# Part of the early rows fetched by SP during the sums, fewer parked by POOL

## The chip, the cores and the metric

One core of one Trainium2 chip runs the whole program. The metric is the device time of one execution in microseconds, the median of the runs. The engines are TensorE (PE), VectorE (DVE), ScalarE (ACT), GpSimd (POOL) and SyncE (SP); each works through its own instructions in order and waits on semaphores for the others. Transfers are issued from SP, ACT and POOL.

## What is computed

A graph convolution with a residual, a mixture of 64 experts of which each node uses two, a norm over all nodes and a norm over each row. There are N = 12500 nodes with D = 256 features and M = 212500 edges, sorted by their target node.

```python
deg_out = clip(segment_sum(ones, src), 1); deg_in = clip(segment_sum(ones, dst), 1)
h = feats * rsqrt(deg_out)[:, None]
m = segment_sum(h[src], dst) * rsqrt(deg_in)[:, None]
x = m @ W_gc + b_gc + feats @ W_res + b_res
y = x + top2_experts(x)
z = (y - mean(y, 0)) * rsqrt(var(y, 0) + eps) * gamma + beta
out = layernorm(feats + z)          # over the features of a node
```

The change lies in the line that makes `m`: for every edge a row of `h`, at the number in `src`, is fetched and added to its target.

## The kernel before

**Stages.** First the degrees of all nodes are counted on PE from one-hot codes that DVE and ACT make. Then x is scaled row by row to `h` and stored in DRAM (`h_d`). Then come the sums over the edges, interleaved with the dense layer, the gating and 20 early tiles of experts. Then the experts, then the two norms.

**Groups of edges.** An edge's source row is fetched by an indirect DMA of POOL, 128 rows of 1 KB at a time; the code calls such a set of 128 edges a row (here: a *row*). There are 1416 rows (`MC`) that POOL gathers from `h_d` during the sums, into a ring of 20 places (L962, in the function `row`). PE multiplies each by a one-hot matrix that DVE made twelve rows ahead (L954, `one_hot`), and adds it into a window of 128 nodes (L976).

**Early rows.** Another 180 rows (`SC`), 90 pairs (`NC2`), are not gathered in the sums. POOL fetches their sources earlier, from x itself, because `h` is not known yet: 140 of them while the degrees are counted (`early_row`, L309), the other 40 right after (`parked`, L746), into 16 buffers of a pair each. SP stores each pair to DRAM (`early_d`, L320 and L773); the parked ones only after the 16 stores of h that stand ahead of them on SP's queue (L768, L770). With more than 16 pairs to park, POOL waits for buffers.

In the sums these pairs come back, one pair for every nine rows (`BATCH`). For a pair, `fetch_again` has SP send the numbers of its 256 sources to all partitions (L1713) and load the rows from `early_d` (L1717). As the rows were taken from x, each must still be multiplied with the scale of its source: DVE makes one-hot codes of the source's low digits (`digits`, L1722), PE looks the scales up (`look_up`, L1730), DVE picks the right one by the high digit (`factors`, L1738) and makes the one-hot codes of the targets (L1745), ACT scales the rows (`scaled`, L1755), and PE adds them up (`sum_again`, L1760). Two buffers alternate, so pair k + 2 is fetched when pair k has been summed.

**Accumulators.** `acc` holds the sums of all nodes, in 14 pieces (`NPW`). A piece is set to zero by SP, which copies zeros from DRAM (`cleared`, L1699; each clear first loads a register, L1692). Before the sums `acc` held x and h. The sums reach the pieces in the order of the nodes, so those of the last nodes are touched last.

**Order.** In the sums the order on PE, DVE, ACT, POOL and SP is written out by hand: `at_row(c, f)` puts a piece of work behind row c of all engines' lists, and each engine then takes its own instructions in that order. So a DMA of SP that is issued "at row 300" stands on SP's queue behind all that was put there before, and waits for nothing but its own semaphores and those ahead of it. Besides the early pairs, SP has there the rows of h that belong to a group's own nodes (`own`, L1002), the stores of finished nodes (L1148) and the weights of the early tiles (L1485). Between the stage of `h` and the sums there is a branch (L795) for inputs that do not fit the windows; it is not taken here. `take` and `hold` share PSUM buffers between the chains.

Of the kernel before, what the change touches and what calls it, by code (L numbers as in the profile page):

```python
# [11 lines left out]
I32 = mybir.dt.int32  # L12
U32 = mybir.dt.uint32
AF = mybir.ActivationFunctionType
ALU = mybir.AluOpType
# [4 lines left out]
P = 128  # L20
N = 12500
D = 256
# [24 lines left out]
HE = HC * P  # L47
BL = 26
# [3 lines left out]
MC = UG * GR  # L52
SR = 15
SB = 4
SG = SB * (NB - 1)
SC = SG * SR
# [3 lines left out]
L = -(-(M - HE - SC * P) // NL // 2) * 2  # L60
# [78 lines left out]
D2 = D + 2  # L139
# [5 lines left out]
def gnn_moe_kernel(  # L145
# [60 lines left out]
    lane = const.tile([P, P], F32)  # L206
# [60 lines left out]
    acc = accp.tile([P, 2 * NP], F32)  # L267
# [9 lines left out]
    src_col = edge.tile([P, NC], I32)  # L277
    rel = edge.tile([P, NC], F32)
# [20 lines left out]
    early = {"wait": []}  # L299
    STORE_LAG = 4  # L300

    def early_row(c):

        while early["wait"] and (early["wait"][0][0] <= c - STORE_LAG):
            stored()
        if c % 2 == 0:
            early["t"] = line.tile([P, 2, D], F32, name="early", bufs=6)
        t = early["t"]
        GP.indirect_dma_start(  # L309
            out=t[:, c % 2],  # L310
            out_offset=None,
            in_=x,
            in_offset=bass.IndirectOffsetOnAxis(ap=src_col[:, MC + c : MC + c + 1], axis=0),
        )
        if c % 2:
            early["wait"].append((c, t))

    def stored():
        c, t = early["wait"].pop(0)
        nc.sync.dma_start(early_d[c // 2], t)  # L320

    def early_rows(to):
        for c in range(early.get("n", 0), min(to, SC)):
            early_row(c)
        early["n"] = max(early.get("n", 0), min(to, SC))
        while early["n"] == SC and early["wait"]:
            stored()

    in_order = tc.manual_schedule(engines={mybir.EngineType.Pool, SP, DVE})
# [2 lines left out]
    with ExitStack() as stack:  # L332
# [226 lines left out]
        for c0 in range(0, C0 + 1, CH):  # L559
            n = min(CH, C0 + 1 - c0)  # L560
# [18 lines left out]
            for k in range(k0, k1):  # L579
                c = k * G  # L580
# [42 lines left out]
        c = C0 + 1 - rest  # L623
# [109 lines left out]
    with ExitStack() as stack:  # L733
# [110 lines left out]
    with ExitStack() as stack:  # L844
# [11 lines left out]
        for i in range(5):  # L856
            r = one.tile([P, RR, D2], F32, name=f"ring{i}")
# [3 lines left out]
        again_ = []  # L861
        for i in range(2):
            r = one.tile([P, 2, D2], F32, name=f"again{i}")
# [13 lines left out]
        p_again = banks[2][:, :D2]  # L877
# [789 lines left out]
        def at_row(c, f):  # L1667
            heapq.heappush(todo, (c, len(given_at), f))
            given_at.append(c)

        def compact_by(c):

            steps_of = squeeze_all()
            lays = [(j, which) for j in range(0, GR, 4) for which in range(2)]
            c -= 3 * len(lays) + 4 + 4 + NL * GR // P + 6
            for i, f in enumerate(steps_of):
                at_row(c * i / len(steps_of), lambda t, f=f: f())
            for i, (j, which) in enumerate(lays):
                at_row(c + 3 * i, lambda t, j=j, w=which: hold(t, lambda t: lay(j, w, t)))
            end = c + 3 * len(lays) + LAG  # L1680
            at_row(end, lambda t: cleared(range(NPW - 4, NPW)))
            for i in range(NB - 1):
                for j in range(NC2 // (NB - 1)):
                    k = i * (NC2 // (NB - 1)) + j
                    fetch_at.append(end + 4 + BATCH * k)
            for k in range(2):
                at_row(fetch_at[k], lambda t, k=k: fetch_again(k, t))

        def cleared(pieces):

            for i in pieces:
                _, u = nc.values_load_multi_w_load_instructions(  # L1692
                    unfit_i[0:1, 0:1],
                    engines=[SP],
                    min_val=0,
                    max_val=1,
                    skip_runtime_bounds_check_because="unfit_i is a comparison",
                )
                nc.sync.dma_start(  # L1699
                    acc[:, i * PW : (i + 1) * PW],  # L1700
                    acc_d[bass.ds(u[0] * (i + 1), 1)].rearrange("a p f -> p (a f)"),
                )
# [4 lines left out]
        def fetch_again(k, t):  # L1707

            i = k * 2
            b, j = divmod(i, SB * SR)  # L1710
            e = HE + b * BE + BL * L + j * P
            wide = spare[:, (3 + k % 2) * D : (4 + k % 2) * D]
            nc.sync.dma_start(  # L1713
                wide.bitcast(I32),
                src[e : e + 2 * P].rearrange("(a c) -> a c", a=1).to_broadcast([P, 2 * P]),
            )
            nc.sync.dma_start(again_[k % 2][:, :, :D], early_d[k])  # L1717
            at_row(t + 4, lambda t: digits(k, wide, t))

        def digits(k, wide, t):  # L1720
            w = wide.bitcast(I32)
            V.tensor_single_scalar(w, w, 127, op=ALU.bitwise_and)  # L1722
            V.tensor_scalar(wide, w, part, None, op0=ALU.is_equal)
            at_row(t + 2, lambda t: hold(t, lambda t: look_up(k, wide, t)))
# [26 lines left out]
        def scaled(k, wide, t):  # L1751
# [3 lines left out]
                S.activation(r[:, i, :D], r[:, i, :D], AF.Copy, scale=factor[:, c : c + 1])  # L1755
            at_row(t + 2, lambda t: sum_again(k, 0, wide, t))

        def sum_again(k, i, wide, t):
            g, j = divmod(2 * k + i, SR)
            T.matmul(  # L1760
                p_again, wide[:, i * P : (i + 1) * P], again_[k % 2][:, i],
                start=j == 0, stop=j == SR - 1,
            )
            if j == SR - 1:
                at_row(t + 2, lambda t: out_of(UG + g, t))
            if i == 1 and k + 2 < NC2:
                at_row(max(t + 1, fetch_at[k + 2]), lambda t: fetch_again(k + 2, t))
            if i == 0:
                if j == SR - 1:
                    at_row(t + 4, lambda t: sum_again(k, 1, wide, t))  # L1770
                else:
                    sum_again(k, 1, wide, t)

        with tc.manual_schedule(engines={
            mybir.EngineType.PE, DVE, mybir.EngineType.Activation, mybir.EngineType.Pool, SP,
        }):
# [15 lines left out]
            at_row(MC - 240, lambda t: x_part(0, t))  # L1792
            at_row(SORT_AT, sort_early)
            at_row(TAKE_AT - 16, lambda t: soon.update(close=True))
            for i in range(EARLY):
                at_row(TAKE_AT + STEP * i, lambda t, i=i: behind(
                    "gated", i - 2, t, lambda t, i=i: early_tile(i, t)
                ))
            compact_by(HC - AHEAD)
            for c in range(AHEAD):  # L1800
                one_hot(c)
            for c in range(MC):
                row(c)
                if c + AHEAD < MC:
                    one_hot(c + AHEAD)
                while todo and todo[0][0] <= c:
                    heapq.heappop(todo)[2](c)
            for i in range(AT_ONCE):
                tc.declare_no_dep(
                    add_early(i, at_e[:, 1]).ins,  # L1810
                    group="late stores",
                    reason="nodes of early tiles were ranked before",
                )
            while todo:
                t, _, f = heapq.heappop(todo)
                f(t)
# [16 lines left out]
    with ExitStack() as stack:  # L1833
# [14 lines left out]
            junk, left, cnt, None, op0=ALU.is_gt, op1=ALU.add, accum_out=pos[:, 0:1]  # L1848
# [23 lines left out]
    with ExitStack() as stack:  # L1872
# [204 lines left out]
        n = EARLY - AT_ONCE  # L2077
# [320 lines left out]
```

## Time and profile before

| | us |
|---|---|
| median of 3 runs | 3549.48 |
| the three runs | 3547.8, 3549.48, 3579.87 |
| the profiled execution | 3578.71 |
| its span, first to last instruction | 3576.9 |
| parking, first to last gather of POOL | 359.03 to 418.93 |
| first product of the sums on PE | 440.51 |
| last gather of the sums starts | 2583.7 |
| busy: PE / PE loads / DVE / ACT / POOL | 2494.7 / 1898.2 / 1797.0 / 826.2 / 2186.7 |

Times in the profile are microseconds from the first instruction, unless marked ns. A line of a group names the line of the kernel, the engine, the operation, the tile written and read, the count, the busy time, the mean of one in ns and the idle time ahead of it with what ended most of it. SPq stands for SP's queue of instructions; PEld are the loads of weights into TensorE. The mean granted clock of TensorE in this execution was 0.821.

### The profile page before, as it was taken

What the parts mean: (1) busy time and instruction counts of PE and PEld (TensorE: products, weight loads), DVE (VectorE), ACT (ScalarE), POOL (GpSimd) and SP (SyncE); (2) the same over time, 40 slices, a digit from 0 to 9 for tenths busy, and PEclk for the clock granted to TensorE, in tenths of its full rate; (3) what the DMA queues carried; (4) which work ended last, traced back from release to release, by engine and by line L of the source; (5) the groups of instructions that cost most, each with busy time, mean ns of one, the idle gap of its engine ahead of it and who ended that gap; (6) DMA issues with size and microseconds to landing.
All of it is one profiled execution on the core that took longest, in us unless ns stands there. A gap on an engine that the chain in (4) does not pass through costs nothing. (4 is left out here: it accounts for less than half of the span.)

```text
span 3576.9 us, 40976 instructions
## 1 busy us (share of the span) xinstructions
PE 2494.7 (70%) x12046; PEld 1898.2 (53%) x12121; DVE 1797.0 (50%) x7367; ACT 826.2 (23%) x2028; POOL 2186.7 (61%) x2169
## 2 busy tenths in 40 slices
PE   2626066566666667676676666578769999999966
PEld 1515033455555545555555455456547767767756
DVE  2829554255455555655455444356643333334347
ACT  1515301122112122121222112122112211211246
POOL 6270777666666666666665666666547777777621
PEclk6657567788787878788788787788889999999988
DMA  7370853455455554555554544445466667667764
GB/s 258 109 235 4 304 191 110 144 146 152 130 144 143 147 142 139 146 140 162 162 162 145 162 152 137 138 144 179 132 171 148 162 150 193 161 173 183 174 168 144
DMA packets 319779, 562.31 MB, mean 157 GB/s; under 512 B 47850, under 2 KB 236366, under 8 KB 308798
## 3 DMA queue, kind: packets, MB, share of 16 engines
q0 software_dynamic: 119456, 266.90, 29.4%
q1 hardware_dynamic: 186555, 279.83, 24.5%
q10 hardware_dynamic: 13539, 12.90, 1.2%
q8 instruction: 99, 1.62, 0.2%
q14 instruction: 130, 1.06, 0.1%
HBM read 455.41 MB, written 105.12 MB: 157 GB/s over the span
## 5 line engine op out<-in xcount | busy, mean ns | idle before, releaser
L962 POOL DMA_INDIRECT ring<-h_d,src_col x1416 | 1364.4, 964 | 748.1 <-issue 385.4
L976 PE MATMUL p<-ring,o 128*128 128x258 f32 x2832 | 899.3, 447 | 175.0 <-DMA ring<-h_d,src_col 97.1
L976 PEld LDWEIGHTS p<-ring,o 128*128 128x128 f32 x2832 | 594.7, 223 | 337.3 <-issue 148.0
L954 DVE TENSOR_SCALAR o<-lane,rel 128x128 f32<-128x128 f32 x1416 | 356.4, 298 | 328.6 <-remote 163.8
L1993 POOL DMA_INDIRECT z_d<-yo,tables x219 | 340.5, 1555 | 146.2 <-issue 48.9
L1983 PE MATMUL yp<-w,h 128*128 128x256 f32 (+7 forms) x1928 | 381.2, 392 | 9.4 <-DVE yo L1987 8.4
L1960 PE MATMUL hp<-xT,w 128*128 128x384 f32 (+22 forms) x1168 | 350.5, 454 | 2.0 <-DVE xT L1951 1.3
L1983 PEld LDWEIGHTS yp<-w,h 128*128 128x128 f32 (+7 forms) x1928 | 296.3, 174 | 71.3 <-issue 17.2
L1964 ACT ACTIVATE h<-hp,w 128x384 f32<-128x384 f32 (+21 forms) x292 | 159.1, 546 | 622.8 <-PE hp L1960 513.7
L1960 PEld LDWEIGHTS hp<-xT,w 128*128 128x128 f32 x1168 | 218.6, 192 | 112.3 <-issue 49.6
L1931 POOL DMA_INDIRECT xg<-x_d,tables x219 | 215.3, 983 | 77.9 <-issue 52.1
L1951 DVE COPY xT<-xtp 128x768 f32<-128x768 f32 (+20 forms) x73 | 63.6, 871 | 329.6 <-PE xtp L1947 295.5
L1755 ACT ACTIVATE again<-again,factor 128x256 f32<-128x256 f32 x180 | 82.4, 502 | 634.2 <-issue 364.3
L309 POOL DMA_INDIRECT early<-in_x,src_col x140 | 149.8, 1070 | 113.4 <-DMA early_d<-early 60.8
L1051 PE MATMUL q<-ident,s 128*128 128x128 f32 x236 | 58.8, 339 | 200.7 <-DVE tables L1738 72.8
L1010 ACT COPY s<-p 128x258 f32<-128x258 f32 x118 | 44.0, 373 | 636.8 <-remote 274.1
L1730 PE MATMUL q<-r_out,tables 128*128 128x98 f32 x360 | 70.1, 327 | 160.0 <-DVE tables L1738 59.0
L591 PE MATMUL deg<-o_hi,o_lo 128*128 128x98 bf16 x1254 | 105.8, 255 | 102.8 <-issue 66.0
L1987 DVE TENSOR_TENSOR yo<-yp,bb 128x256 f32<-128x256 f32 (+6 forms) x219 | 92.9, 424 | 162.5 <-PE yp L1983 132.4
L589 ACT ACTIVATE s_lo<-lane_b,nb 128x128 bf16<-128x128 bf16 x396 | 122.1, 388 | 201.6 <-PE deg_s L593 96.0
L1730 PEld LDWEIGHTS q<-r_out,tables 128*128 128x128 f32 x360 | 65.7, 238 | 177.3 <-issue 74.4
L1051 PEld LDWEIGHTS q<-ident,s 128*128 128x128 f32 x236 | 35.2, 171 | 234.4 <-DVE tables L1738 79.5
(428 smaller groups left out, 3853.0 us busy)
## 6 DMA issues: line engine op xcount, KB each, us to landing
w<-in_wpack SPq DMA_DIRECT2D x64, 1026.0 KB
again<-early_d SPq DMA_DIRECT2D x90, 256.0 KB
ring<-h_d,src_col POOLq DMA_INDIRECT x1416
acc<-in_wpack SPq DMA_DIRECT2D x20, 1026.0 KB
early_d<-early SPq DMA_DIRECT2D x70, 256.0 KB
tables<-h_d SPq DMA_DIRECT2D x104, 128.0 KB
acc<-acc_d SPq DMA_DIRECT2D x14, 896.0 KB
acc<-in_x SPq DMA_DIRECT2D x12, 1024.0 KB
```

The costliest lines, as they stand in the source:

```text
L309: GP.indirect_dma_start(out=t[:, c % 2], out_offset=None, in_=x, in_offset=bass.IndirectOffsetOnAxis(ap=src_col[:, MC + c : MC + c + 1], a ...
L589: S.activation(s_lo[:, i], lane_b, AF.Sign, bias=nb[:, k - k0, i : i + 1])
L591: T.matmul(deg, o_lo[:, i], o_hi[:, i], start=c + i == 0, stop=False)
L954: o_last[u] = V.tensor_scalar(o_of[u][:, j], lane, rel[:, c : c + 1], None, op0=ALU.is_equal)
L962: i = GP.indirect_dma_start(out=r[:, k, :D], out_offset=None, in_=h_d, in_offset=bass.IndirectOffsetOnAxis(ap=src_col[:, c : c + 1], axis=0),)
L976: i = T.matmul(p_of[g], o_of[v][:, n], r[:, k], start=j == 0, stop=j == GR - 1)
L1730: T.matmul(p_r[:, i], wide[:, i * P : (i + 1) * P], r_out, start=True, stop=True)
L1931: i = GP.indirect_dma_start(out=g[:r], out_offset=None, in_=x2_d, in_offset=bass.IndirectOffsetOnAxis(ap=at[:r, 0, k : k + 1], axis=0),)
L1960: T.matmul(hp[:, :m], w1[:, c, j * P : (j + 1) * P], xT[:, c, :m], start=c == 0, stop=c == 1,)
L1964: S.activation(h1[:, j, :m], hp[:, :m], AF.Gelu, bias=w[:, 2 * H + 4 * D + j : 2 * H + 4 * D + j + 1],)
L1983: T.matmul(yp, h1[:, j, a : a + r], w2[:, j], start=j == 0, stop=j == 3)
L1993: st = GP.indirect_dma_start(out=z_d, out_offset=bass.IndirectOffsetOnAxis(ap=at[:r, 1, k : k + 1], axis=0), in_=yo, in_offset=None, compu ...
```

## The change

Sixteen of the early rows, the eight pairs 19, 29, ... 89 (`LONE`), are no longer fetched from x by POOL. The list of the other 82 pairs (`GATHERED`, 164 rows) takes the place of all pairs in `early_row`, `stored` and `parked`. The stage of the degrees still fetches 140, so 24 rows are parked in place of 40, and all 12 pairs have a buffer at once.

The rows of the eight pairs are fetched during the sums by SP, from `h_d`, where they are scaled already. SP reads the numbers of the sources in chunks of 64 into one partition (`lone_load`), loads four of them into registers (`lone_quad`), and issues a copy of one row of 1 KB for each: 2048 copies, 512 register loads and 32 loads of chunks. One group of four is put behind every 1.7 rows, from row 6 on. The rows land in two pieces of `acc` (6 and 13) that the sums reach late: six places of a pair, so the last two pairs use places 0 and 1 again after their sums. These two pieces are cleared at row 1030, the others as before.

`fetch_again` of such a pair sends nothing, and digits, look-up, factors and scaling fall away for it; DVE makes the one-hot codes of its targets (`lone_ones`), and PE takes the rows from their place in `acc`. As such a pair is ready sooner, `sum_again` now keeps the sums in order with a counter.

```diff
+LONE = [19 + 10 * i for i in range(8)]
+GATHERED = [k for k in range(NC2) if k not in LONE]
+NGA = 2 * len(GATHERED)
+QUAD, CHUNK = 4, 64
+LONE_FROM, LONE_STEP = 6, 1.7
...
-        pairs = list(range(early["n"] // 2, NC2))
+        pairs = GATHERED[early["n"] // 2 :]
...
-            at_row(end, lambda t: cleared(range(NPW - 4, NPW)))
+            at_row(end, lambda t: cleared(range(NPW - 4, NPW - 1)))
...
+            if k in LONE:
+                at_row(t + 8, lambda t: lone_ones(k, wide, t))
+                return
...
+        def lone_load(n):
+            if n < len(LONE) * 2 * P // CHUNK:
+                e = lone_edges(n)
+                nc.sync.dma_start(
+                    lone_ix[n % 2], src[e : e + CHUNK].rearrange("(a c) -> a c", a=1)
+                )
+
+        def lone_quad(q):
+            n, a = divmod(q * QUAD, CHUNK)
+            if a == 0:
+                lone_load(n + 1)
+            _, v = nc.values_load_multi_w_load_instructions(
+                lone_ix[n % 2][0:1, a : a + QUAD],
+                engines=[SP],
...
+            k, r = divmod(n * CHUNK + a, 2 * P)
+            i, p = divmod(r, P)
+            for j in range(QUAD):
+                nc.sync.dma_start(
+                    rows_of(LONE[k])[p + j : p + j + 1, i, :D], h_d[bass.ds(v[j], 1)]
+                )
+
+        def lone_ones(k, wide, t):
+            for i in range(2):
+                c = 2 * k + i
+                V.tensor_scalar(
+                    wide[:, i * P : (i + 1) * P], lane, rel[:, MC + c : MC + c + 1], None,
+                    op0=ALU.is_equal,
+                )
+            at_row(t + 2, lambda t: sum_again(k, 0, wide, t))
...
+        summed = [0, 0]
+
         def sum_again(k, i, wide, t):
+            if 2 * k + i > summed[0] or t < summed[1]:
+                at_row(t + 1, lambda t: sum_again(k, i, wide, t))
+                return
+            summed[0] += 1
             g, j = divmod(2 * k + i, SR)
+            if j == SR - 1:
+                summed[1] = t + 4
             T.matmul(
-                p_again, wide[:, i * P : (i + 1) * P], again_[k % 2][:, i],
+                p_again, wide[:, i * P : (i + 1) * P], rows_of(k)[:, i],
                 start=j == 0, stop=j == SR - 1,
             )
...
             cleared([0, NPW // 2])
-            for i in range(1, NPW // 2):
+            for r in lone_home:
+                V.memset(r[:, :, D : D + 1], 1.0)
+                V.memset(r[:, :, D + 1 :], 0.0)
+            lone_load(0)
+            for q in range(len(LONE) * 2 * P // QUAD):
+                at_row(LONE_FROM + int(LONE_STEP * q), lambda t, q=q: lone_quad(q))
+            at_row(1030, lambda t: cleared([NPW // 2 - 1, NPW - 1]))
+            for i in range(1, NPW // 2 - 1):
```

More of the change, by code (lines that the diff above doesn't have):

```diff
@@ L312, in early_row @@
             in_=x,
[L313 removed]
+            in_offset=bass.IndirectOffsetOnAxis(ap=src_col[:, a : a + 1], axis=0),
         )
@@ L319, in stored @@
         c, t = early["wait"].pop(0)
-        nc.sync.dma_start(early_d[c // 2], t)
+        nc.sync.dma_start(early_d[GATHERED[c // 2]], t)
     def early_rows(to):
-        for c in range(early.get("n", 0), min(to, SC)):
+        for c in range(early.get("n", 0), min(to, NGA)):
             early_row(c)
-        early["n"] = max(early.get("n", 0), min(to, SC))
-        while early["n"] == SC and early["wait"]:
+        early["n"] = max(early.get("n", 0), min(to, NGA))
+        while early["n"] == NGA and early["wait"]:
             stored()
@@ L1718, in fetch_again, with rows_of, lone_edges @@
             at_row(t + 4, lambda t: digits(k, wide, t))
+        lone_home = [
+            acc[:, (p + 1) * PW - PW + i * 2 * D2 : (p + 1) * PW - PW + (i + 1) * 2 * D2].rearrange(
+                "p (i d) -> p i d", d=D2
+            )
+            for p in (6, 13)
+            for i in range(PW // (2 * D2))
+        ]
+        lone_ix = [
+            acc[0:1, 7 * PW - (i + 1) * CHUNK : 7 * PW - i * CHUNK].bitcast(I32) for i in range(2)
+        ]
+        def rows_of(k):
+            return lone_home[LONE.index(k) % len(lone_home)] if k in LONE else again_[k % 2]
+        def lone_edges(n):
+            k, m = divmod(n, 2 * P // CHUNK)
+            b, j = divmod(2 * LONE[k], SB * SR)
+            return HE + b * BE + BL * L + j * P + m * CHUNK
+        def lone_load(n):
[11 more added lines that the diff above has]
+                engines=[SP],
+                min_val=0,
+                max_val=N - 1,
+                skip_runtime_bounds_check_because="src holds numbers of nodes",
+            )
[4 more added lines that the diff above has]
+                    rows_of(LONE[k])[p + j : p + j + 1, i, :D], h_d[bass.ds(v[j], 1)]
+                )
+        def lone_ones(k, wide, t):
[4 more added lines that the diff above has]
+                    op0=ALU.is_equal,
+                )
+            at_row(t + 2, lambda t: sum_again(k, 0, wide, t))
         def digits(k, wide, t):
```

1 line of the change is left out of this document (added).

## The prediction

> **What bounds the kernel now.** I read the page first, then the timeline of POOL and SP around 360 to 460 us, then the waits of SP, DVE and PE in the stretch in which the new copies would run.
>
> ```profile
> span 3576.9 us, 40976 instructions
> ...
> q1 hardware_dynamic: 186555, 279.83, 24.5%
> ...
> L962 POOL DMA_INDIRECT ring<-h_d,src_col x1416 | 1364.4, 964 | 748.1 <-issue 385.4
> ```
>
> Over 2,100 us of the span is the stage of the sums, and POOL's 1416 gathers from h are its clock: each is followed by a pause that no wait explains. Ahead of that stage lies the parking, which the change shortens:
>
> ```profile
> 359.03 0.96 POOL L746 DMA_INDIRECT park<-in_x,src_col  x1 [93.30 <-DVE r_out L241]
> ...
> 395.77 0.94 POOL L746 DMA_INDIRECT park<-in_x,src_col  x1 [0.30 <-issue]
> ...
> 407.66 0.95 POOL L962 DMA_INDIRECT ring<-h_d,src_col  x1 [0.30 <-issue]
> ...
> 418.93 0.94 POOL L746 DMA_INDIRECT park<-in_x,src_col  x1 [0.30 <-issue]
> 420.18 0.95 POOL L962 DMA_INDIRECT ring<-h_d,src_col  x1 [0.30 <-issue]
> ```
>
> The row at 395.77 is the 24th park. Thirty-two parks run to 407.3, then two ring gathers, then the last eight parks, which need a buffer that SP has emptied; from 420.18 on the ring runs alone. A step (0.95 and a pause of 0.30) is 1.25 us. POOL waits for nothing else, so it sets when the sums begin:
>
> ```profile
> 439.54 2.64 DVE L954 TENSOR_SCALAR o<-lane,rel 128x128 f32<-128x128 f32 x13 [38.25 <-DMA ring<-h_d,src_col]
> ```
> ```profile
> 440.51 2.06 PE L976 MATMUL p<-ring,o 128*128 128x258 f32 x4 [66.74 <-DMA ring<-h_d,src_col]
> ```
>
> Both engines stand at the branch of the rare case until the gathers that were issued before it have landed. What POOL gains ahead of this point, the sums begin earlier. SP and the DMA engines in the same stretch:
>
> ```profile
> 359.19 38.16 SPq L768 DMA_DIRECT2D h_d<-acc  x15
> 397.45 2.67 SPq L770 DMA_DIRECT2D h_d<-acc  x1
> 400.29 24.54 SPq L773 DMA_DIRECT2D early_d<-park  x20
> ...
> 458.90 2.85 SPq L1699 DMA_DIRECT2D acc<-acc_d  x4
> ```
> ```profile
> 415.00:420.00 5.00, 0.00 (x0) 0.00 (x0) 0.00 (x0) 0.00 (x0) 3.79 (x4) 0.50 1.01 377
> 430.00:440.00 10.00, 0.00 (x0) 0.00 (x0) 0.46 (x3) 0.00 (x0) 7.58 (x8) 0.50 0.42 119
> ```
>
> (The last two columns are the busy share of the 16 DMA engines and GB/s.) They are full until 420 and half idle once the parks are done.
>
> In the sums, rows come slower than POOL could give them:
>
> ```profile
> 640.00:1770.00 1130.00, 711.94 (x744) 0.81 0.51 147
> ```
>
> That is 1130/744 = 1.52 us a row, against a step of 1.25. Nine rows, the distance between two early pairs, are 13.7 us. The rest is lost in handshakes, and SP stands in one of them: it may send for the sources of the next early pair (L1713) only when PE has summed an older one, and DVE's digits (L1722) wait for that transfer.
>
> **The change part by part.**
>
> *Parking.* Sixteen gathers and eight stores go. 16 x 1.25 = 20 us is the most. But the ring needs the whole of h, whose last store leaves SP at 397.45 + 2.67 = 400.1 with the DMA engines full. POOL is done with 24 parks at 396.7, so it now waits for h. Before, the ring effectively began two steps ahead of 420.18, at 417.7. If h lands no earlier than the first ring gather shows (407.66), the gain is 10 us; if it lands 2.4 us after its issue (402.5), 15. I take 13: 24 fewer transfers share the full engines, so h should land a little sooner than before.
>
> *Eight pairs leave the handshake.* No source broadcast, no load from the parked copy, no digits, look-up, factors or scaling for them. What the look-ups hold up on PE, from the waits between 645 and 1770:
>
> ```profile
> PE q L1051 <- DVE tables L1738: 91.6, 17, 17.5
> PE q L1730 <- DVE tables L1738: 59.0, 7, 11.8
> PE q L1730 <- DVE tables L1722: 32.4, 5, 12.1
> ```
>
> 183 us over the 79 pairs of that stretch, 2.3 us a pair; eight pairs are 18.5 us at most, and nothing if the next instruction in PE's order waits in its place. I take 12. The pieces of work themselves (ACT and DVE are each busy half the time or less there) cost the path nothing beyond this.
>
> *The copies.* 512 groups of four: one register load, then four times address, move and a copy of one row of 1 KB; 2048 copies in all, plus 32 small loads of indices. They stand on SP's queue from row 6 to row 876, one group for each 1.7 rows. The rows for their price:
>
> ```profile
> L994 SPq TENSOR_LOAD <-n_row x27: 296/305/480, 647.9 to 2570.6; - x27
> ```
> ```profile
> L1692 SPq TENSOR_LOAD <-unfit_i x14: 3/270/701, 437.5 to 644.6; - x14
> ```
> ```profile
> L1002 SPq FUSED_REGOPS  x104: 3/37/718, 648.5 to 2577.8; - x104
> L1002 SPq MOVE tables<-h_d x104: 2/29/846, 648.6 to 2577.9; - x104
> L1002 SPq DMA_DIRECT2D tables<-h_d x104: 3/346/1077, 649.1 to 2578.0; - x104
> ```
> ```profile
> L419 SPq DMA_DIRECT2D tables<-in_src x1: 256/256/256, 147.9 to 147.9; - x1
> L419 SPq DMA_DIRECT2D l_dst<-in_dst x1: 223/223/223, 150.1 to 150.1; - x1
> ```
>
> The four clears at 458.90 come one after the other: (2.85 - 0.34)/3 = 0.84 us for one load and one copy. Of this 270 + 37 + 29 + 346 ns are the instructions, so 40 ns lie between two of them. No dynamic copy of one row stands in the trace. Its nearest row is L419, one partition and one piece, 0.24 us; the other end is the copy of 128 rows with a register, 0.346. With 0.24 a copy is 37 + 29 + 240 + 3 x 40 = 426 ns and a group 305 + 40 + 4 x 426 = 2.05 us; with 0.346 it is 2.47 us.
>
> *What covers them.* SP issues in order and waits much. Between 645 and 1770:
>
> ```profile
> SPq L1713 <- PE bank L1760: 149.8, 25, 15.5
> SPq L1713 <- remote: 147.6, 17, 15.7
> SPq L1148 <- DVE top L1235: 133.1, 15, 19.1
> SPq L1713 <- DVE tables L1745: 103.6, 15, 15.3
> SPq L1713 <- PE p L976: 84.7, 8, 25.9
> SPq L1148 <- DVE ahead L1286: 62.8, 10, 13.3
> SPq L1148 <- remote: 19.7, 2, 10.9
> SPq L1713 <- PE bank L1279: 15.2, 1, 15.2
> SPq L1713 <- DVE o L954: 12.9, 1, 12.9
> ```
>
> 729 of 1125 us. Rows 160 to 876 fall in this stretch and carry 421 groups: 863 us. If the other 396 us are SP's own work, the sum is 1259 us and SP is 134 us too slow. If they are not (each early pair costs SP two issues,
>
> ```profile
> L1713 SPq DMA_DIRECT2D tables<-in_src x90: 3/328/700, 645.5 to 1879.0; - x90
> L1717 SPq DMA_DIRECT2D again<-early_d x90: 3/524/827, 646.0 to 1879.5; - x90
> ```
>
> about 1 us with the steps, and own rows and node stores about half a microsecond each, together some 150 us), then 863 + 150 = 1013 us still fit, at nine tenths of SP's time.
>
> The first 91 groups (rows 6 to 156, 187 us) and the clears fill the time in which SP stood at the last clears, from 462 to about 643, and cost nothing while those clears wait as long as now.
>
> *What is late next.* SP no longer arrives at L1713 ahead of its release but behind some groups of copies. Queued behind them are the sources of the next early pair, and for these waits DVE, already now:
>
> ```profile
> DVE tables L1722 <- DMA tables<-in_src: 96.4, 23, 12.2
> ```
>
> In 23 of 79 pairs DVE has no time in hand. One group (2.05 us) ahead of each of 72 remaining pairs is 148 us of later landings; 23/79 of it, 43 us, reaches DVE, and of DVE's 96.4 us PE showed 32.4, a third: 15 us. That is the lower end, the 134 us of the overfull queue the upper. I take the middle, 75: the queue is in order, its releases come bunched, and nine tenths of a queue's time cannot be used without being late often.
>
> The Trainium skill, page "Perfetto Trace Analysis", section "DMA Instruction — HWDGE (DVE, Sync)", says that a semaphore wait of such a copy is spent on the issuing sequencer before the copy's recorded start. The trace agrees: SP's waits above stand apart from issues of 0.3 to 0.5 us. By that rule the copies behind a blocked L1713 do not slip past it, as the sum assumes.
>
> *Sum.* -13 - 12 + 75 = +50 us. On the profiled execution, 3578.71 us with a span of 3576.9, that is 3629; the median of the runs is 29 us lower, and 3549.5 + 50 = 3599.5. A measurement of this kernel can tell about 1%, 35 us, from no change.
>
> **The rivals.**
>
> *SP keeps up.* The 2.05 us groups fit into its waits, and DVE's time in hand hides what comes late. For it: the 1013 us above fit into 1125, and 56 of 79 pairs had time in hand. Against it: 23 had none. The result is the gains alone, 25 less a few: 3530 us, and 3510 if parking gives 15 and the eight pairs their full 18.5 and some of their work. This is the other side; it decides as long as a group costs under (1125 - 150)/421 = 2.3 us and the releases are even.
>
> *SP saturates.* If a copy of one row with a register costs SP as much as one of 128 rows, a group is 2.47 us, 421 are 1040 us, and 396 + 1040 = 1436 is 311 more than the stretch: 3835 us. For it: the only copies with a register in the trace cost 0.346. Against it: L419.
>
> *One DMA engine.* Suppose that all these one-piece copies run on one of the 16 engines, and that a gather is finished only with its slowest. From the page, a packet of q1 takes 0.245 x 16 x 3577/186555 = 75 ns, so a group takes 0.3 of its 2.05 us on that engine, which was busy for half the time (0.51 above) and would be at two thirds. Unless bursts fill it, nothing happens. If they do, POOL's issues lengthen: by 0.2 us on 870 rows, 174 us, it ends at 3700. The Trainium skill, page "DMA: Bandwidth & Descriptors", section "Why a DMA increments its semaphore by 16 and not by 1", says that a one-piece copy runs on one engine, the lowest-numbered; no run here shows which engine a copy took.
>
> *The parking gives nothing back.* The gathers wait for h as long as the parks took: 3549.5 + 75 - 12 = 3612.
>
> **How the numbers follow.** Forecast 0.45 (its own range 3540 to 3660, from 15 and 134 us of loss), SP keeps up 0.33, SP saturates 0.12, one engine 0.05, no gain from parking 0.05. Faster by over 1% (under 3514) is a third of the second case: 0.12. Within 1%: the rest of that case and a third of the forecast, 0.37. Slower: 0.51. The range leaves out the best of the second case and nearly all of saturation: 3512 to 3720.
>
> **What would show it.** Right: 24 parks, first ring gather about 404, first sum at 425 to 430; SP's waits on L1713 shrink from hundreds of microseconds to tens; DVE's wait for the sources grows well over 100 us in the rows up to 876; rows there take 1.6 us instead of 1.52 and the old pace afterwards. Wrong: SP's waits on L1713 stay above 100 us and the row pace is 1.5 or less (SP keeps up); or SP is never idle and rows take 1.8 us (saturation); or POOL's gathers themselves lengthen (one engine).

## The result: 15% slower, and the profile after

The changed kernel takes 4098.77 us (median of 6 runs, 4088.57 to 4101.47) against 3551.9 us for the kernel before (6 runs): a ratio of 1.152, 95% interval 1.149 to 1.156. The forecast was 3599.5 us, its range 3512 to 3720. The profiled execution took 4101.47 us; from its page:

```profile
span 4099.7 us, 47579 instructions
...
POOL 6423772145444344444444566666654677777741
...
DMA  7635342133333333333333555544555666777674
...
L968 POOL DMA_INDIRECT ring<-h_d,src_col x1416 | 1359.3, 960 | 1301.2 <-PE p L982 603.4
...
L1784 DVE TENSOR_SCALAR tables<-tables 128x256 int32<-128x256 int32 x82 | 24.8, 303 | 950.7 <-DMA tables<-in_src 925.3
```

POOL's gathers (L962 before, now L968) last as long as before, 960 against 964 ns, but POOL stands still ahead of them for 1301 us in place of 748. DVE's digits (L1722 before, now L1784) wait 925 us for the sources of the early pairs. The row of POOL has a hole in its seventh and eighth slice and stays at 3 to 5 tenths to the 22nd. The same gathers by stretch (columns: length, POOL busy and count, TensorE clock, DMA share, GB/s):

```profile
640.00:800.00 160.00, 10.27 (x11) 0.50 0.18 62
800.00:1600.00 800.00, 371.67 (x391) 0.73 0.36 102
...
2300.00:2600.00 300.00, 179.23 (x188) 0.82 0.54 165
```

Eleven rows in 160 us, then 2.05 us a row, and after the last copy (2305 us) 1.60. The issue that DVE waits for stands on SP's queue, and this is SP, first by what it waited for between 640 and 2300 us, then by the instructions of the copies:

```profile
SPq L1769 <- DMA acc<-h_d: 17.7, 37, 1.4
...
SPq L1722 <- PE p L982: 1.3, 4, 0.4
```
```profile
L1769 SPq FUSED_REGOPS  x2048: 2/37/728, 426.1 to 2305.1; - x187
L1769 SPq MOVE acc<-h_d x2048: 1/29/1405, 427.5 to 2305.2; - x187
L1769 SPq DMA_DIRECT2D acc<-h_d x2048: 2/228/1395, 428.9 to 2305.3; - x187
```
```profile
L1759 SPq TENSOR_LOAD <-acc x512: 2/554/1384, 424.0 to 2303.3; - x171
```

SP hardly waits for anyone any more: the hundreds of microseconds ahead of the fetch of sources (L1713 before, now L1722) are 1.3. The three numbers behind a colon are the shortest, median and longest duration in ns. The medians of the three instructions of a copy are near those of the forecast (37, 29 and 240), that of the load is not (554 against 305). The longest are twenty to fifty times the median for the register operations and MOVEs and six times for the copies, and they decide, as two pieces of SP's timeline show, with POOL's gathers in the same two windows:

```profile
546.86 28.06 SPq L1769 DMA_DIRECT2D acc<-h_d  x11
...
713.20 18.04 SPq L1769 DMA_DIRECT2D acc<-h_d  x32
```
```profile
546.80:574.90 28.10, 17.36 (x19) 0.68 0.34 100
713.20:731.30 18.10, 0.00 (x0) 0.50 0.16 53
```

The same instructions: 11 copies in 28 us beside 19 gathers of POOL, 32 copies in 18 us while it stands. In the first window most instructions (20 of 31), register operations and MOVEs among them, start 0.7 or 1.4 us after the one ahead; in the second they take 37, 29 and 228 ns with some 40 ns between them.

Where the time went, from the starts of PE's sums in the two traces (us; the last column is the end of the span):

| | row 0 | row 100 | row 160 | row 876 | row 1415 | end |
|---|---|---|---|---|---|---|
| before | 440.5 | 566.6 | 662.2 | 1754.6 | 2597.1 | 3576.9 |
| after | 422.4 | 551.0 | 796.6 | 2292.5 | 3133.7 | 4099.7 |

The sums begin 18.1 us earlier. Rows 100 to 160 take 150.0 us longer, rows 160 to 876 take 403.5 us longer (1495.9 against 1092.4), and everything else together 12.6 us less: 523 us in all.

From here a group is one register load with its four copies, and its price the time of SP's unbroken strings of groups, from the start of the first load to the end of the last copy, divided by their groups. Sorted by how busy POOL was with gathers during a string, the 512 groups of the kernel after cost:

| POOL busy | under 5% | 5 to 30% | 30 to 60% | over 60% | mean |
|---|---|---|---|---|---|
| us a group (groups) | 2.35 (127) | 2.51 (61) | 3.22 (173) | 4.27 (151) | 3.23 |

Rows 160 to 876 hold 418 loads in the trace; 418 groups at 3.06 us (their mean there) are 1279 us of 1495.9, and 217 us are left for everything else that SP issues or waits for. Of SP's waits the trace shows 39 us in all between 640 and 2300 us, so SP's time is the length of the stretch.

### The profile page after: what moved, and what is told of

It is laid out like the page before. It is cut to its first block, busy times and chain, and to the rows that moved or that the text cites. A ratio compares the mean times of both kernels' runs of the same rounds, so it can differ in the third digit from the quotient of the medians.

```text
span 4099.7 us, 47579 instructions
## 1 busy us (share of the span) xinstructions
PE 2528.4 (62%) x12089; PEld 1915.3 (47%) x12089; DVE 1778.4 (43%) x7331; ACT 818.6 (20%) x2012; POOL 2159.0 (53%) x2153
## 5 line engine op out<-in xcount | busy, mean ns | idle before, releaser
L968 POOL DMA_INDIRECT ring<-h_d,src_col x1416 | 1359.3, 960 | 1301.2 <-PE p L982 603.4
L982 PE MATMUL p<-ring,o 128*128 128x258 f32 x2832 | 915.7, 456 | 147.1 <-DMA ring<-h_d,src_col 79.0
L982 PEld LDWEIGHTS p<-ring,o 128*128 128x128 f32 x2832 | 613.2, 230 | 308.7 <-issue 140.8
L1784 DVE TENSOR_SCALAR tables<-tables 128x256 int32<-128x256 int32 x82 | 24.8, 303 | 950.7 <-DMA tables<-in_src 925.3
L1194 PE MATMUL q<-ident,xt 128*128 128x128 f32 x190 | 34.8, 314 | 235.0 <-issue 193.5
L597 PE MATMUL deg<-o_hi,o_lo 128*128 128x98 bf16 x1254 | 104.6, 251 | 121.1 <-issue 82.2
```

The lines of the kernel that those rows point to most:

```text
L597: T.matmul(deg, o_lo[:, i], o_hi[:, i], start=c + i == 0, stop=False)
L968: i = GP.indirect_dma_start(out=r[:, k, :D], out_offset=None, in_=h_d, in_offset=bass.IndirectOffsetOnAxis(ap=src_col[:, c : c + 1], axis=0),)
L982: i = T.matmul(p_of[g], o_of[v][:, n], r[:, k], start=j == 0, stop=j == GR - 1)
```

## The experiments

The runs come in series, each with its own runs of the kernel before on the same chip; ratios are to these, and their median is named where it is far from 3.55 to 3.6 ms. Runs without an interval are single ones; what is read from them are prices of a group and effects of 100 us and more.

**The copies taken away, or their parts.** In the first run the quads are never issued, and DVE fills the sixteen rows with a constant:

```
-            lone_load(0)
-            for q in range(len(LONE) * 2 * P // QUAD):
-                at_row(LONE_FROM + int(LONE_STEP * q), lambda t, q=q: lone_quad(q))
+            for i, r in enumerate(lone_home):
+                at_row(20 + 4 * i, lambda t, r=r: V.memset(r[:, :, :D], 0.5))
```

> The 2048 copies and their 512 register loads are left out (the 16 rows of the eight pairs hold a constant); parking, accumulators and the order of the sums stay as in the kernel after. Theory A (SP's time for the copies is the whole loss): the time falls below the kernel before by the two gains of the prediction, 13 us of parking and 12 us of digits and look-ups, so 3515 to 3545 us against 3552. Theory B (the new order of the sums, or the late clearing of the two pieces, costs by itself): above 3600 us with SP mostly idle.

Measured: ratio 0.997, interval 0.993 to 1.001 (3581.89 against 3593.56 us). The copies are the whole loss. What is left is 12 us, half of the forecast 25 and not clear of zero. Rows 160 to 876 take 1109.9 us here, no less than before, so what gain there is lies ahead of the sums (67.5 us from the first park to the first sum, 81.5 before), and nothing shows that eight pairs fewer in the handshake have bought anything. DVE waits for the sources as before:

```profile
  DVE tables L1784: 100.7, 30
```

(who waited for SP's fetch, in us and times). The second run has the copies read fixed rows and drops the register load (its lines are left out here), so that no load, register operation or MOVE stands ahead of them:

```
...
-                    rows_of(LONE[k])[p + j : p + j + 1, i, :D], h_d[bass.ds(v[j], 1)]
+                    rows_of(LONE[k])[p + j : p + j + 1, i, :D], h_d[q * QUAD + j : q * QUAD + j + 1]
```

> The 2048 one-row copies stay, but from fixed rows of h: no TENSOR_LOAD, FUSED_REGOPS or MOVE in front of them (the rows fetched are the wrong ones). Theory A (every instruction of SP is drawn out beside POOL's gathers, so a group costs by its number of instructions): a group falls from 3.23 us to 1.3 to 2.0 us, 512 of them take 670 to 1020 us, SP keeps up, and the time is 3520 to 3620 us. Rival B (issuing or landing of the copies is what is slow, the register work rides along): a group stays above 2.8 us and the time above 3950 us.

Measured: a group falls from 3.23 to 2.05 us, and rows 160 to 876 take 1135.5 us. The other rows lead the later stage into 512 more POOL gathers, so the whole time (7692 us) says nothing; the expectation of 3520 to 3620 us could not be read. The price fell with the number of instructions, as the first theory had it, though not quite so far. Four copies alone cost 1.42 us a group where POOL is idle and 2.34 where it is over 60% busy: the copies too are drawn out.

```profile
L1762 SPq DMA_DIRECT2D acc<-h_d x2048: 2/250/1439, 437.1 to 1868.9; - x187
```

The third run was to have the loads alone:

> The 512 register loads of four source numbers each stay, the 2048 copies with their FUSED_REGOPS and MOVE are left out (the 16 rows hold a constant). Theory A: a load costs 0.6 to 0.8 us, 512 of them 310 to 410 us of SP, which has 729 us of waiting in rows 160 to 876; 3515 to 3560 us. Rival C (the register loads, waiting for memory, hold SP up): above 3650 us.

Measured: 3579.11 us, a ratio of 0.996. It doesn't test the loads: with their values unused, the trace has 512 short semaphore instructions in their place and no load at that line. It stands as a second run without copies: rows 160 to 876 take 1119.7 us in it.

**Half the copies.** `LONE = [29 + 20 * i for i in range(4)]` and `LONE_STEP = 3.4`.

> Four pairs in place of eight, a group of four copies every 3.4 rows in place of 1.7; POOL parks 32 rows. Theory A with the price at full gathering (4.27 us a group where POOL is busy over 0.6 of the time): 256 groups take 1090 us beside some 400 us of SP's other work in 1400 us, just over the edge: 3560 to 3680 us. With the mean price of the kernel after (3.23 us) SP would keep up and the gains would show: 3530 to 3560 us. Rival D (each copy costs the sums a fixed share, 549 us over 2048 copies): 3552 + 274 = 3826 us.

Measured: 1.029, interval 1.020 to 1.038 (3697.65 us; 18 us above the expected 3560 to 3680). A group costs 4.31 us in the mean, as the price at full gathering foretold: POOL gathers for more of the time than in the kernel after, and each group is dearer. SP is still all but without waits from 660 to 1880 us, and a loss in proportion to the copies (3826 us) is ruled out:

```profile
SPq L1722 <- PE bank L1830: 19.5, 8, 7.7
SPq L1769 <- DMA acc<-h_d: 13.3, 29, 1.4
SPq L1722 <- remote: 11.9, 7, 6.2
```

**POOL's gathers replaced.** In one run POOL fills the ring with memsets, in the other it gathers 64 bytes of each row:

```
-            i = GP.indirect_dma_start(
-                out=r[:, k, :D],
-                out_offset=None,
-                in_=h_d,
-                in_offset=bass.IndirectOffsetOnAxis(ap=src_col[:, c : c + 1], axis=0),
-            )
+            i = GP.memset(r[:, k, :D], 0.5)
```
```
-                out=r[:, k, :D],
+                out=r[:, k, :16],
                 out_offset=None,
-                in_=h_d,
+                in_=h_d.rearrange("n (a b) -> (n a) b", b=16),
```

> The kernel after with POOL's 1416 ring gathers of the sums replaced by as many POOL memsets of the same ring rows (the sums are then over constants, and what follows the sums is not comparable; only SP's price of a group up to the last copy is read). Theory A (POOL's gathers draw SP's instructions out): a group of four copies costs 2.3 to 2.6 us in every stretch, as it did in the kernel after where POOL stood still (2.35 us). Rival B (SP's own stream, its queue or the landing of its copies is what is slow): 3.0 us or more, as in the kernel after (3.23 us).

> The kernel after with the ring gathers fetching 64 bytes of each of the 128 rows in place of 1024 (the sums are over other data, and what follows them is not comparable; only SP's price of a group is read). If it is the running of the gathers on POOL that draws SP out, a group stays at 3.0 to 3.6 us with POOL's gather at 0.9 us or more. If it is the bytes on the DMA engines, it falls to 2.3 to 2.6 us.

Measured, in one series on one chip: 2.44 us a group without gathers, 3.29 us with thin ones (2.35 us in the strings with POOL under 5%, 4.41 over 60%). The instructions of the copies without gathers:

```profile
L1764 SPq FUSED_REGOPS  x2048: 37/37/47, 423.0 to 1863.8; - x187
L1764 SPq MOVE acc<-h_d x2048: 29/29/39, 423.1 to 1863.9; - x187
L1764 SPq DMA_DIRECT2D acc<-h_d x2048: 219/228/305, 423.1 to 1863.9; - x187
```

and with thin gathers, and those gathers:

```profile
L1770 SPq FUSED_REGOPS  x2048: 1/37/1403, 439.4 to 2356.8; - x187
L1770 SPq MOVE acc<-h_d x2048: 1/29/1407, 440.2 to 2356.8; - x187
```
```profile
L969 POOL DMA_INDIRECT ring<-h_d,src_col x1416: 939/947/1515, 417.5 to 3189.1; - x177
```

Not one of 6144 instructions is drawn out without gathers. With a sixteenth of the bytes and gathers of the same length, all comes back. Later in the run without gathers, where POOL gathers for the experts, SP's register operations are drawn out again:

```profile
L1956 SPq FUSED_REGOPS  x64: 3/37/719, 2497.9 to 3251.5; - x64
```

So what draws them out was there in this run too, and needs POOL's gathers; the bytes that these move are not it. Whether the number of their pieces, 128 each, matters was not tried.

**The rows fetched by POOL in place of SP**, a version that the first result suggests: two gathers from h for each of the eight pairs, in POOL's own order some 70 rows ahead of their sum; then the same for 20 pairs, with nothing left to park.

```
+        def lone_fetch(k):
+            for i in range(2):
+                a = MC + 2 * k + i
+                GP.indirect_dma_start(
+                    out=rows_of(k)[:, i, :D],
+                    out_offset=None,
+                    in_=h_d,
+                    in_offset=bass.IndirectOffsetOnAxis(ap=src_col[:, a : a + 1], axis=0),
+                )
...
+            for k in LONE:
+                at_row(90 + 9 * k, lambda t, k=k: lone_fetch(k))
```

> A version of its own: the same eight pairs, each fetched by two POOL gathers from h into the same accumulators some 70 rows ahead of its sum, no copies and no register loads on SP. 16 gathers of 0.96 us are 15 us of POOL, which gathers 0.64 of the time there. Theory A: as without copies, a ratio of 0.993 to 1.000. Rival: a POOL gather more delays every ring gather behind it and all 15 us show: 1.000 to 1.004.

> As the version before, with 20 pairs in place of eight, so that POOL parks no row and 40 gathers from h stand between the ring gathers; 20 pairs leave digits and look-ups. The ring can't start sooner than h is stored, which the kernel after had already waited for 9 us, so the start gains nothing more; if the handshakes of 12 more pairs pay as forecast (1.5 us a pair), 18 us less than with eight pairs, a ratio of 0.988 to 0.996; if they pay nothing, the same as with eight pairs or up to 0.004 more.

Measured: 1.003 (1.000 to 1.007) and 1.008 (1.005 to 1.011). The rivals held: rows 160 to 876 take 1129.7 us with 16 gathers more and 1148.8 with 40, that is 20 and 39 us above the first run without copies (10 and 29 above the second), near a microsecond a gather. That POOL stands for a third of the stretch doesn't make a gather free. Nor did 12 pairs fewer in the handshake pay for anything that shows.

**Another queue, another start, fewer pairs.** The four runs of one series: all groups issued by ACT (`engines=[mybir.EngineType.Activation]`, `nc.scalar.dma_start`), four pairs' groups issued by ACT, all groups on SP but from row 160 (`LONE_FROM, LONE_STEP = 160, 1.4`), and two pairs on SP (`LONE = [49 + 40 * i for i in range(2)]`, `LONE_STEP = 6.8`).

> The kernel after with the 512 register loads and 2048 copies of the eight pairs issued by ACT in place of SP. In the traces so far ACT's own DMA issues beside POOL's gathers all took 374 to 397 ns, SP's instructions alone were drawn out. Theory A (the drawing out is SP's): a group takes 2.4 to 2.9 us on ACT with no instruction of 0.7 us; 512 of them 1230 to 1480 us beside ACT's own 200 us, more than the 1315 us of rows 0 to 876: 3620 to 3850 us. Rival E (whatever engine issues beside POOL's gathers is drawn out): 3.0 us a group or more and above 3950 us.

> Four pairs in place of eight, their 256 groups every 3.4 rows issued by ACT. Theory A: 256 groups of 2.4 to 2.9 us are 610 to 740 us beside ACT's 200 us in 1315 us, ACT keeps up, and only a wait of up to one group ahead of some evictions is left: a ratio to before of 0.995 to 1.012, against 1.029 from SP. Rival E: 256 groups at 4.3 us as on SP, 1.02 to 1.04.

> The kernel after with the same 512 groups on SP begun at row 160 in place of row 6, one every 1.4 rows. Theory A (SP's time is what sets the pace, and the first stretch only put off its work): the stand of 150 us between rows 100 and 160 goes, and rows 160 to 876 take 512 x 3.06 + 196 = 1760 us in place of 1496: some 4210 us. Rival F (the loss is caused by the first stretch, where POOL gathers without a pause and a group took 5 to 8 us, and what piles up there): 3950 us or less.

> Two pairs in place of eight, one group on SP every 6.8 rows; POOL parks 36 rows. Theory A: 128 groups at the price of full gathering, 5.2 us, are 660 us of SP in 1315 us and SP keeps up; the parking of four rows less gives 3 us: a ratio of 0.996 to 1.004. Rival D (each copy costs the sums a fixed share): 549 x 2 / 8 = 137 us, 1.038.

In this series the kernel before took 3088.06 us (14 runs), and the times have to be read against that; the expected times had been written for 3.55 ms. Measured: 3455.28 us (1.119), 0.994 (0.992 to 0.996), 3563.63 us (1.154), 0.997 (0.995 to 0.999). The trace shows what was different. SP's 512 groups of the late start, beside POOL's gathers at full length:

```profile
L1769 SPq FUSED_REGOPS  x2048: 37/37/47, 459.5 to 1881.0; - x187
L1769 SPq MOVE acc<-h_d x2048: 29/29/42, 459.6 to 1881.1; - x187
L1769 SPq DMA_DIRECT2D acc<-h_d x2048: 219/228/385, 460.2 to 1881.2; - x187
```

No instruction is drawn out, a group costs 2.41 us whether POOL is idle (2.36) or over 60% busy (2.43), and in the run of two pairs the sums begin at 294.9 us and rows 160 to 876 take 911.0 us. So gathers on POOL are needed for the drawing out, but they are not enough; something outside the kernel goes with it. And SP's bare time is a loss without it: rows 160 to 876 took 1387.6 us, 477 us above two pairs, and 512 groups at 2.41 us are 1234 us of them, more than two pairs needed for everything. ACT's price was about 2.7 us a group; 512 of them and ACT's 200 us overfill rows 0 to 876, and ACT's own work for the sums waits behind them (PE waits 365 us there for ACT's L977).

**The same again where SP is drawn out.** The next series, on a chip of the same number, gave the kernel before 3579.72 us; so it is not the chip's number that decides.

> The kernel after as it is. Chips differ: where the kernel before takes 3.55 to 3.6 ms, SP's instructions were drawn out beside POOL's gathers, and where it took 3.09 ms none was (512 groups at 2.41 us). If this chip is of the first kind, a ratio of 1.14 to 1.16 with 3.2 us a group. If of the second: the sums' rows 160 to 876 take 911 us there without many copies, 421 groups at 2.41 us and 196 us of SP's other work make 1211 us, 300 us more, and the first 91 groups, 219 us, fit into the first 160 rows' 190 us nearly: a ratio of 1.10 to 1.13. If the drawing out were the whole cause, the second kind would show 1.00 to 1.03.

> Four pairs, their 256 groups issued by ACT, on a chip again. Where SP is drawn out: if ACT is not drawn out there either, ACT keeps up as it did and the ratio is 0.985 to 1.005 against 1.029 from SP; if ACT is drawn out like SP, 1.02 to 1.04. On a chip where SP is not drawn out: 0.99 to 1.00 as measured before.

> All 512 groups issued by ACT. Where the sums' rows take 1.53 us a row (SP drawn out), rows 0 to 876 have 1310 us; 512 groups at 2.4 to 2.7 us and ACT's own 195 us make 1430 to 1580 us: 100 to 270 us over, a ratio of 1.03 to 1.08, half or less of the loss from SP. If ACT is drawn out like SP: 1.15 or more. On a chip without drawing out, 1.119 as measured.

> The 512 groups on SP from row 160, one every 1.4 rows. Where SP is drawn out: the stand of 150 us between rows 100 and 160 goes, rows 160 to 876 take 512 x 3.06 + 196 = 1760 us, some 120 us above the kernel after of the same chip (ratio to before 1.17 to 1.20). If the loss comes from the first stretch: 1.11 or less. On a chip without drawing out: 1.154 as measured.

Measured: 1.158 (1.149 to 1.166), 1.019 (1.010 to 1.028), 3940.94 us (1.101), 4204.56 us (1.175). The kernel after shows its price again (3.26 us a group, 2.35 with POOL idle, 4.34 over 60%). The late start did as SP's time foretold: rows 100 to 160 took 93.9 us, the stand of 150 us was gone, rows 160 to 876 took 1719 us (1760 expected), and the whole was 60 us longer than the kernel after in this series. The stand was put-off work, no cause of its own. The same kernel, the same lines as in the fence above:

```profile
L1769 SPq FUSED_REGOPS  x2048: 2/37/1401, 643.5 to 2392.8; - x187
L1769 SPq MOVE acc<-h_d x2048: 1/29/1394, 643.5 to 2392.8; - x187
L1769 SPq DMA_DIRECT2D acc<-h_d x2048: 1/228/1417, 644.2 to 2393.5; - x187
```

ACT is not spared, and both results for it lie between the cases of their expectations:

```profile
L1769 ACTq FUSED_REGOPS  x2048: 2/37/1393, 436.0 to 2140.6; - x187
L1769 ACTq MOVE acc<-h_d x2048: 2/29/785, 436.1 to 2140.6; - x187
```

But it is drawn out less: while a gather runs, 7% of ACT's register operations reach the next instruction only after more than 0.45 us, 16% of SP's in the kernel after of this series; a group costs about 3.0 us on ACT. Eight pairs lose two thirds as much from ACT as from SP; with four pairs the intervals of 1.019 and 1.029 overlap.

**Two pairs there.**

> Two pairs, 128 groups on SP every 6.8 rows, POOL parks 36 rows; a chip where the kernel before takes 3088 us gave 0.9973. Theory A where SP is drawn out: 128 groups at 5.2 us are 670 us in the 1310 us of rows 0 to 876, SP keeps up, but a pair's digits can come one group (5 to 8 us) late: a ratio of 0.996 to 1.006. If a pair's digits behind SP's groups cost the sums more than that: 1.01 or more, half of the 1.029 of four pairs.

Measured: 0.998, interval 0.996 to 1.001, with 5.10 us a group. The loss goes 15.8%, 2.9%, 0 with eight, four and two pairs: it ends where SP keeps up (312 us of waits between 670 and 1777 us, 69 between 660 and 1880 with four pairs). No version was clearly better than the kernel before where SP is drawn out; four pairs on ACT (0.994) and two on SP (0.997) were where it is not.

## Why the prediction was wrong, point by point

**Parking: right.** From the first park to the first sum, 81.5 us before and 66.3 us after, a gain of 15.2 us (13 forecast, 10 to 20 as bounds). The ring starts at 402.95 us (404 forecast), after the wait for h that the forecast had put there (the row names a store of parked rows; POOL's long semaphore wait ahead of it ends at 402.14, when the last store of h, issued at 394.11, has landed):

```profile
392.91 0.95 POOL L752 DMA_INDIRECT park<-in_x,src_col  x1 [0.30 <-issue]
402.95 0.94 POOL L968 DMA_INDIRECT ring<-h_d,src_col  x1 [9.09 <-DMA early_d<-park]
```

**Eight pairs leave the handshake, -12 us: not found.** Without copies, rows 160 to 876 took 1110 and 1120 us against 1092. The lower bound, that the next instruction waits in the place of the one removed, was nearer.

**The price of a group: the step that failed.** The forecast was 2.05 us, from medians and from a one-piece copy of 0.24 us. The copy was right (228 ns), the gaps nearly, the load not (554 ns against 305), which gives the 2.35 us of an idle POOL. The load of L994 was no bad choice: it reads four numbers too. The same load takes longer where copies stand among its neighbours, in the late start without drawing out as well (first row, against 308 ns in the run without copies, second row):

```profile
L1000 SPq TENSOR_LOAD <-n_row x27: 301/550/797, 478.7 to 2543.4; - x27
L1000 SPq TENSOR_LOAD <-n_row x27: 298/308/527, 636.5 to 2571.7; - x27
```

The rest, up to 3.23 us in the mean and some 8 between 500 and 650 us, is the drawing out, and it stood in the rows quoted for the price: their longest durations were 701, 718, 846 and 700 ns where the medians were 270, 37, 29 and 328. They are not outliers: in the trace of the kernel before, 10 of the 104 register operations and 20 of the 104 MOVEs of L1002 took over 300 ns, and their means are 86 and 142 ns. With these two means in place of the medians the forecast's own sum gives 2.70 us a group, and 421 of them 1137 us, more than the whole stretch of 1125: a saturated queue.

The Trainium skill, page "Perfetto Trace Analysis", section "DMA Instruction — HWDGE (DVE, Sync)", counts the wait for the descriptor block's lock into a copy's record, which could stretch a copy. FUSED_REGOPS and MOVE issue no copy, and the trace has them at 0.7 and 1.4 us too, so that wait doesn't account for them.

**The first 91 groups, costing nothing: wrong.** They had the 219 us up to the late clears, in which they were to take 187. At 5 to 12 us a group only 32 were begun by 640 us; most of the others came ahead of the first early pair's sources (fetched at 787 us), with PE and POOL standing, and cost the 150 us.

**The cover, 729 us of SP's waits: right in kind.** SP's other work and waits were 217 us, between the 150 and 396 of the text. With 2.41 us a group the stretch would have been 421 x 2.41 + 217 = 1232 us, 140 above before, near the upper end of +134 that the forecast carried; with 3.06 it was 403 above.

**The rivals.** "SP saturates" named what happened: SP is never idle and everything behind it is late. It was priced from one copy of 0.346 us at 3835 us and given 0.12; its reason was another, and its size 264 us short. "One DMA engine" fell: the gathers' 960 ns did not grow. "The parking gives nothing back" fell with the 15.2 us. "SP keeps up" was to hold under 2.3 us a group; it held with a quarter of the groups, at 5.10 us each.

**What would show it.** Three signs of the forecast came, and saturation would have brought them too: the wait on sources above 100 us for DVE, SP's waits ahead of it down to a few, and the old pace after row 876. The fourth, the row pace, told them apart: 2.09 us for rows 160 to 876 was beyond both the forecast's 1.6 and the 1.8 of saturation.

The Trainium skill, page "DMA: Bandwidth & Descriptors", section "Issuing engines are not separate DMA queues", says that starting transfers from several engines saves only the sequencer's time for starting them, usually small beside the transfer. Here that time was the loss: four copies of 1 KB with their register load cost their queue 2.35 us at the least, and by the updates of their semaphores half of the copies land within about 1.2 us of the end of their issue.

## What to carry to other kernels

Price an instruction stream of a queue with the means and the longest durations in its rows as well as with the medians, and ask which other engine was running when they were long. Many small copies cost the queue that issues them, and everything ordered behind them, long before they cost the DMA engines: sum the queue's own instructions against its recorded waits, and keep well below. When a stage has a slack engine, a change that leans on it can find the slack gone in the very stretch where another engine speeds up.

## What the runs showed of the hardware that was not expected

- SP's instructions, register operations among them, take about 0.7 or 1.4 us each in part of the time that POOL runs indirect gathers, in the first pair of traces and in all series but one. Replaced by memsets, the gathers leave 37 and 29 ns; at 64 bytes a row the effect is unchanged. ACT shows it more weakly.
- In one series none of it was there with the same gathers, and the kernel before took 3088 us in place of 3550 to 3600. What makes the difference is open; a later series on a chip of the same number had the drawing out. The medians are 37 and 29 ns in both, so it is not that SP is slower throughout. Every execution here has a recorded span and clock, so whether the recording plays a part can't be told either.
- The kernel before bears part of it too. The kernel with two pairs has a trace of each kind, with spans of 3080.6 and 3585.8 us: 156 of the 505 us between them lie ahead of the first sum, and 196 in rows 160 to 876, where a row takes 1.27 us, close to POOL's step of 1.25, in place of 1.55. So the 0.27 us a row above that step, which the prediction put down to handshakes, are all but absent in that series. Ahead of the sums, beside POOL's early gathers, PE stands for 96.3 us without a wait that the trace shows (L597) in the slower one and DVE with it; DVE between 50 and 100 us (busy and count, TensorE clock, DMA share, GB/s), first without, then with the drawing out:

```profile
50.00:100.00 50.00, 49.31 (x100) 0.72 0.88 273
50.00:100.00 50.00, 2.79 (x4) 0.50 0.79 263
```

That the drawing out is all of the 505 us is not shown. It is open too what the change would cost without it: the nearest run is the late start, 1.154.
- A register load of four numbers takes 305 ns on SP in the kernel before and 550 with single-row copies among its neighbours (L994 and L1000 above); why is open.
